# A graph attention layer and a gated graph recurrence on one core: adjacency loaded with a cast to float16 and turned by transposing transfers, nodes counted (k p)

## Chip, cores and metric

One core of a Trainium2 chip. The metric is device time in microseconds (us) of the whole kernel, the median of several executions. Lower is better. The engines are named as in the profile: PE (TensorE, with PEld for its weight loads), DVE (VectorE), ACT (ScalarE), POOL (GpSimd) and SP (SyncE, which only issues transfers here).

## The reference

There are 32 sequences (graphs) of 512 nodes with 128 features; all share one 512 x 512 adjacency matrix of zeros and ones.

```
# layer 0: graph attention
h = relu(layernorm(x))
hw = h @ W;  e_src = hw @ a_src;  e_dst = hw @ a_dst
logits = leaky_relu(e_src[i] + e_dst[j], 0.2), masked by A[i, j] > 0
x = x + leaky_relu(softmax_j(logits) @ hw + b, 0.3)
# layer 1: five steps of a gated recurrence
h = relu(layernorm(x))
repeat 5 times:
    m = A @ h                       # in_matrix and out_matrix are both A
    z = sigmoid([m, m] @ w3.T + w3_b + h @ u3.T + u3_b)
    r = sigmoid([m, m] @ w4.T + w4_b + h @ u3.T + u3_b)
    v = tanh([m, m] @ w5.T + w5_b + (r * h) @ u5.T + u5_b)
    h = (1 - z) * h + z * v
x = x + h
```

## The kernel before

**Layout.** P is 128 partitions, N 512 nodes, K = 4 blocks of 128 nodes, D 128 features. A sequence lies in the local memory either by nodes (partition = a node of a block, `[P, K, D]`) or turned (partition = a feature, `[P, N]`). Nodes are counted "(p k)": partition p holds nodes 4p to 4p+3, so one load of `x` reads 2 KB in one piece for each partition. The adjacency is loaded in float32 as `a_sb` (L415), and must then be turned: `prepare_adjacency` (L487) makes each of four blocks by four PE transposes (L494) into one bank of the accumulator memory, and copies them as float16 to `adjT` (L503, ACT for even, DVE for odd blocks).

**Layer 0** (`layer0`, L769) for each sequence: a norm (statistics L621, aggregate L629, `pow` on POOL L650, then for sequence 0 centring and scaling on DVE, L659 and L665, and for others a relu with scale on ACT, L687); a turn of the normed features; the product `hp` with W and the two attention vectors (L812); exponentials (L818) and scaled rows (L825); `es`, the row of exponentials spread over all partitions (L847); `pt`, the masked weights (L897, reads `es` and `adjT`); the averages `av` (L928); division, bias, leak and sum with x (L955 to L982), giving `x1`; and a second norm, whose result is `hN` and its two float16 halves `hi` (ACT, L1014) and `lo` (DVE, L1012). Turns and spreads are made by PE for the first DIRECT = 4 sequences, and for the others by a DVE block transpose and transfers through HBM from POOL's queue (`blockwise`, L723).

**The recurrence** (`recurrence`, L1018) for each step: `m` is made of four float16 matmuls with `hi` and four with `lo` against `adjT` (L1037), then copied to `mT` (ACT, L1048); `gate_r` is two float32 matmuls (L1056, L1057), `tanh` of it (ACT, L1062), `rh` (DVE, L1069), `gate_z` one matmul into the same bank (L1077), tanh (L1089), the candidate `v` two matmuls (L1100, L1101), tanh (L1107), and the update on DVE in three steps (L1114, L1120, L1123). The new state is split again and its halves are turned by transposing transfers from SP (`crossed`, L1231, L1245). The last sequences end with PE transposes; the last step of the last two sequences ("near") and of the last one (`ending`, L1256) have forms of their own. In `ending` the candidate is made in two halves of 256 columns in one bank, and the result is turned and summed by PE: four matmuls of the kept part against a scaled negative identity (`minus`, L1276) and four of the new part against a scaled identity (`plus`, L1306), accumulated in another bank.

**The order of work.** No order is written by hand. Each piece of work is a `Task` with an engine, an estimated duration, a key (its priority), the tasks that it needs and the buffers that it takes (L70). `plan` (L88) runs through all tasks with the costs of `COST` (L42) and puts each engine's tasks into one fixed order, which the kernel then issues. A transfer's `lands` is the estimate from its issue to its arrival. Where PE has nothing to do by this plan, filler matmuls on constants (`idle`, L443, 68 in all) are put in. Each engine works strictly in its order; an instruction that waits holds up all behind it on its engine, and a load that waits holds up SP's queue.

**The start.** SP's queue: x of sequence 0, `a_dst`, the adjacency, x of 1 and 2, the weights (`load_rest`, L410), five bias columns, x of 3 and so on. ACT's queue: `gw` (W) and `a_src`, both as columns.

**Sizes that matter:** ten sequences have slots for their state at a time; `d`, the buffer of the update on DVE, has 2 copies; the `pow` of both norms is on POOL, in its order with the transfers that POOL issues.

Of the kernel before, what the change touches and what calls it, by code (L numbers as in the profile page):

```python
# [28 lines left out]
DIRECT = 4  # L29
SHORT = 0  # L30
# [6 lines left out]
ADJ_LANDS = 5600  # L37
HALVED = 1
NEAR = 2
# [10 lines left out]
LANDING = 5000  # L50
CROSSING, CROSSED = 1250, 1400
# [7 lines left out]
    "hv": 2, "d": 2, "way": 4, "turn": 4, "line": 4, "hiT": 3, "loT": 3,  # L59
# [229 lines left out]
def gat_then_gated_gnn_kernel(  # L289
# [26 lines left out]
    x_r = x.rearrange("b (p k) d -> b p k d", k=K)  # L316
    out_r = out.rearrange("b (p k) d -> b p k d", k=K)
# [26 lines left out]

    ident = const.tile([P, P], F32, name="ident")
# [36 lines left out]
    prep = fast.enter_context(tc.tile_pool(name="prep", bufs=1))  # L382
    a_sb = prep.tile([P, K, N], F32, name="a_sb")
    gw = prep.tile([P, D], F32, name="gw")
    gwT = prep.tile([P, D], F32, name="gwT")
    acols = prep.tile([P, 2], F32, name="acols")
    cols = prep.tile([P, 5], F32, name="cols")
    sums2 = prep.tile([P, 2], F32, name="sums2")
    half = const.tile([P, 2], F32, name="half")
    nc.vector.memset(half, 0.5)  # L390
    wa = prep.tile([P, 2], F32, name="wa")
    wide = {name: prep.tile([P, 2 * D], F32, name=name) for name in ("w3", "w4", "w5")}
# [15 lines left out]
    nc.scalar.dma_start(out=acols[:, 0:1], in_=g_asrc.rearrange("(d o) -> d o", o=1))  # L408

    def load_rest(name):  # L410
        if name == "a_dst":
            pin(nc.sync.dma_start(out=acols[:, 1:2], in_=g_adst.rearrange("(d o) -> d o", o=1)))
            return
        if name == "a":
            pin(nc.sync.dma_start(out=a_sb, in_=adj.rearrange("(p k) m -> p k m", k=K)))  # L415
            return
# [8 lines left out]
        nc.sync.dma_start(out=bias0, in_=g_b.partition_broadcast(P))  # L425
# [3 lines left out]
    a_dst_loaded = add("SP", [1], -9.85e9, lambda: load_rest("a_dst"), lands=2900)  # L429
    a_loaded = add("SP", [1], -9.8e9, lambda: load_rest("a"), lands=ADJ_LANDS)  # L430
    xs[1] = load_x(1, -9.7e9, 5000)
    xs[2] = load_x(2, -9.6e9, 5100)
    rest_loaded = add("SP", [1] * 6, -9.5e9, lambda: load_rest("rest"), (xs[2][1],), lands=3000)
# [27 lines left out]

    def issue():
        pin(nc.tensor.matmul(new(f_wa, "wa_ps")[:, 0:2], lhsT=gwT, rhs=acols, start=True, stop=True))

    t = add("PE", [256], soon, issue, (a_dst_loaded, t), (f_wa,), at=5000)
# [17 lines left out]

    adjacency = []

    def prepare_adjacency(c):

        f = Buffer("g", "bank")
        key = (0.2 * c - 3.8) * STEP

        def turn():
            at_ps = new(f, f"at_ps{c}")
            for k in range(K):
                pin(nc.tensor.transpose(  # L494
                    at_ps[:, ts(k, P)],
                    a_sb[:, k, :].rearrange("p (q c) -> p c q", c=K)[:, c, :],
                    ident,
                ))

        t = add("PE", [256] * K, key, turn, (a_loaded,), (f,), at=9900 if c > 1 else 0)  # L500
        engine, copy = ("DVE", nc.vector.tensor_copy) if c % 2 else ("ACT", nc.scalar.copy)
        adjacency.append(
            add(engine, [512], key, lambda: pin(copy(adjT[:, c, :], f.tile)), (t,), (f,))  # L503
        )

    for c in range(K):
        prepare_adjacency(c)


# [45 lines left out]
    late = 5 * (B - 3) * STEP  # L555

    def count(k):
        f = Buffer("d")

        def issue():  # L560
            pin(nc.vector.scalar_tensor_tensor(
                new(f, f"odd_{k}"), a_sb[:, k, :], 0.0, a_sb[:, k, :], ALU.not_equal,
                ALU.not_equal, accum_out=counts[:, k : k + 1],
            ))

        return add("DVE", [512], late, issue, (adjacency[-1],), (f,), at=late)

    def degree(k):
# [5 lines left out]
        return add("DVE", [512], late, issue, (adjacency[-1],), at=late)  # L574
# [25 lines left out]


    def relu_layernorm(dst, src, which, keys, needs, buffers, first):
# [52 lines left out]
        if first:  # L655

            def centre():
# [14 lines left out]
            t1 = add("DVE", [512], keys(2), centre, (t1,), buffers)  # L672
            return [add("DVE", [256], keys(3), scale(i), (t, t1), buffers) for i in range(2)]

# [24 lines left out]
    def transposed(dst, src, which, keys, needs, buffers, by_halves):  # L699

        f = Buffer("o", "bank")

        def turn(half):
            def issue():
                t_ps = f.tile or new(f, f"t_{which}")
# [5 lines left out]
        def copy(of):  # L711
            return lambda: pin(nc.scalar.copy(dst()[:, of], f.tile[:, of]))

        t = [add("PE", [256] * 2, keys(0), turn(i), (needs[i],), (*buffers, f)) for i in range(2)]
        if not by_halves:
            t = add("ACT", [512], keys(1), copy(slice(0, N)), t, (*buffers, f))
            return [t, t]
        return [
            add("ACT", [256], keys(1), copy(ts(i, N // 2)), (t[i],), (*buffers, f))
# [3 lines left out]
    def blockwise(dst, src, which, keys, needs, buffers, by_halves):  # L723
# [23 lines left out]
        for g in range(G):  # L747
            stores.append(add("POOL", [1], keys(1), store(g), (t,), (f, way),
                              lands=LANDING))
# [7 lines left out]
        return add("POOL", [1], keys(2), load, stores, (*buffers, way), lands=LANDING + 1500)  # L757
# [11 lines left out]
    def layer0(b):  # L769
# [7 lines left out]
        def keys(i):  # L777
            return begin + length * (base[0] + i) / parts
# [12 lines left out]
        turn = transposed if direct else blockwise  # L791
# [11 lines left out]
        def product(half):  # L803
# [12 lines left out]

            def exponentials():
                pin(nc.scalar.activation(  # L818
                    hw()[:, 2 * half : 2 * half + 2, D:], hp2()[:, :, D:], AF.Exp
                ))  # L820
# [576 lines left out]
```

## Time and profile before

| what | value |
|---|---|
| median of 3 executions | 1137.68 us (1136.31 to 1139.9) |
| the profiled execution's own time | 1136.34 us |
| its span in the trace | 1134.6 us |
| DVE, ACT, POOL busy | 77%, 58%, 31% of the span |
| f32 gate and candidate matmuls (five lines, L1056 to L1101) | 814.4 us of summed durations |
| f16 matmuls with `hi` and `lo` (L1037) | 322.6 us of summed durations |
| transfers, mean | 92 GB/s, 104.52 MB |
| load of x, 256 KB, issue to landing | 2.9 us |
| transposing transfer from SP, issue to landing | 2.6 us |
| load of the adjacency, 1024 KB | 5.5 us |

Durations of matmuls in the trace overlap, since they are pipelined, so their sum is larger than the span; distances between starts are what they cost. "Idle before" beside a group is the time its engine waited ahead of it, and the releaser is what ended the wait. Times in the timeline count from the span's start.

### The profile page before, as it was taken

The numbers are of one execution on the slowest core, as the hardware profiler recorded it, in microseconds if no ns is written. First come the engines' busy times: TensorE is split into PE (matmuls) and PEld (weight loads), VectorE is DVE, ScalarE is ACT, GpSimd is POOL, SyncE is SP. The second block draws the span as 40 slices with busy tenths as digits, with TensorE's granted clock in tenths as the row PEclk, the third lists the DMA queues.
The fourth block names the chain that finished last, engine by engine and source line by source line (L and its number), as shares of the span: only waits on it lengthen the run. The fifth ranks groups of instructions, "written<-read, shape, count | busy, mean of one in ns | idle before, by whom it ended". The sixth has DMA issues, their size and how long they took to land.

```text
span 1134.6 us, 14335 instructions
## 1 busy us (share of the span) xinstructions
PE 1127.7 (99%) x4334; PEld 592.6 (52%) x4334; DVE 875.4 (77%) x2002; ACT 661.5 (58%) x1299; POOL 351.5 (31%) x504
## 2 busy tenths in 40 slices
PE   9999999999999999999999999999999999999998
PEld 8655555455455545555544555555555554444444
DVE  7888968887687788879777777889888976745655
ACT  6756656645655565656566556665656564555553
POOL 4255432511431344244134214453544230100000
PEclk9999999999999999999999999999999999999999
DMA  3245453643444554355345345454655343331321
GB/s 108 57 88 112 84 108 84 126 88 84 105 81 102 85 121 93 86 120 106 89 102 107 73 100 103 111 101 114 117 116 103 75 76 84 47 74 29 84 74 67
DMA packets 188498, 104.52 MB, mean 92 GB/s; under 512 B 152192, under 2 KB 167680, under 8 KB 188288
## 3 DMA queue, kind: packets, MB, share of 16 engines
q1 hardware_dynamic: 170512, 66.57, 25.4%
q0 software_dynamic: 17472, 36.79, 17.6%
q8 instruction: 36, 0.59, 0.2%
q14 instruction: 46, 0.38, 0.1%
q10 hardware_dynamic: 432, 0.20, 0.1%
HBM read 39.46 MB, written 30.47 MB: 62 GB/s over the span
## 4 chain that ended last, share of the span: by engine, by line
PE 99%; DMA 0%; DVE 0%; SPq 0%; issue 0%; DVEq 0%
PE m L1037 24%; PE g L1077 12%; PE g L1057 12%; PE g L1056 12%; PE v L1101 12%; PE v L1100 12%; PE av L928 10%; PE hp L812 3%; DMA a_sb<-in_adj_dram 0%; PE idle L443 0%; PE at_ps L494 0%; PE t_b L707 0%; PE t_a L707 0%; PE es L847 0%; PE v_end L1288 0%; PE end L1306 0%
## 5 line engine op out<-in xcount | busy, mean ns | idle before, releaser
L1062 ACT ACTIVATE rs<-g,zrb 128x512 f32<-128x512 f32 x160 | 109.6, 685 | 122.7 <-PE g L1057 121.9
L1114 DVE SCALAR_TENSOR_TENSOR d<-hv,hT 128x512 f32<-128x512 f32 x158 | 108.2, 685 | 92.9 <-ACT hv L1107 91.9
L1107 ACT ACTIVATE hv<-v,vb 128x512 f32<-128x512 f32 x159 | 108.8, 684 | 106.6 <-PE v L1101 106.3
L1069 DVE SCALAR_TENSOR_TENSOR rh<-rs,hT 128x512 f32<-128x512 f32 x160 | 109.5, 685 | 71.2 <-ACT rs L1062 70.5
L1056 PE MATMUL g<-hT,u3T 128*128 128x512 f32 x320 | 163.4, 592 | 0.0
L1057 PE MATMUL g<-mT,w4sT 128*128 128x512 f32 x320 | 163.4, 592 | 0.0
L1077 PE MATMUL g<-mT,w3dT 128*128 128x512 f32 x320 | 162.8, 593 | 0.0
L1101 PE MATMUL v<-rh,u5hT 128*128 128x512 f32 x318 | 162.4, 592 | 0.0
L1100 PE MATMUL v<-mT,w5sT 128*128 128x512 f32 x318 | 162.4, 592 | 0.0
L1037 PE MATMUL m<-adjT,hi 128*128 128x512 f16 x640 | 161.9, 379 | 0.0
L1037 PE MATMUL m<-adjT,lo 128*128 128x512 f16 x640 | 160.7, 379 | 0.0
L650 POOL TENSOR_TENSOR rs_b<-ve_b,mhalf 128x4 f32<-128x4 f32 x32 | 36.9, 1154 | 384.2 <-DVE ve_b L630 161.4
L1089 ACT ACTIVATE zs<-g,zrb 128x512 f32<-128x512 f32 x160 | 109.4, 685 | 68.0 <-PE g L1077 66.7
L1048 ACT COPY mT<-m 128x512 f32<-128x512 f32 x160 | 92.9, 583 | 81.7 <-PE m L1037 79.1
L928 PEld LDWEIGHTS av<-hw,pt 128*128 128x128 f32 x1024 | 123.5, 191 | 21.1 <-issue 17.5
L928 PE MATMUL av<-hw,pt 128*128 128x129 f32 x1024 | 125.0, 275 | 0.1
L1123 DVE SCALAR_TENSOR_TENSOR hT<-d,hT 128x512 f32<-128x512 f32 x158 | 109.3, 692 | 11.9
L1237 ACT CAST hiT<-hT 128x512 f16<-128x512 f32 x128 | 78.9, 616 | 66.2 <-DVE hT L1123 64.2
L1037 PEld LDWEIGHTS <-hi 128*128 128x128 f16 x640 | 62.6, 98 | 98.6 <-issue 45.0
L1120 DVE SCALAR_TENSOR_TENSOR d<-zs,d 128x512 f32<-128x512 f32 x158 | 109.2, 691 | 5.2
L1037 PEld LDWEIGHTS <-lo 128*128 128x128 f16 x640 | 62.6, 98 | 90.5 <-issue 25.3
L1240 DVE TENSOR_TENSOR loT<-hT,hiT 128x512 f16<-128x512 f32 x128 | 87.6, 687 | 17.7 <-ACT hiT L1237 16.3
(141 smaller groups left out, 1351.7 us busy)
## 6 DMA issues: line engine op xcount, KB each, us to landing
x<-in_x_dram SPq DMA_DIRECT2D x32, 256.0 KB, 2.9
out_dram<-res SPq DMA_DIRECT2D x31, 256.0 KB, 2.3
turn_a<-blocks_a POOLq DMA_DIRECT2D x112, 64.0 KB, 2.7
h0T<-turn_a POOLq DMA_DIRECT2D x28, 256.0 KB, 4.0
es<-line POOLq DMA_DIRECT2D x28, 256.0 KB, 4.3
turn_b<-blocks_b POOLq DMA_DIRECT2D x112, 64.0 KB, 2.6
hT<-turn_b POOLq DMA_DIRECT2D x28, 256.0 KB, 3.9
way<-blocks SPq DMA_DIRECT2D x28, 256.0 KB, 2.3
```

The costliest lines, as they stand in the source:

```text
L928: pin(nc.tensor.matmul(avs()[:, i, :], lhsT=f_pts[c].tile[:, ts(2 * part + i, P)], rhs=hw()[:, c, : D + 1], start=start, stop=(c == K - 1) ...
L1037: pin(nc.tensor.matmul(f_m.tile, lhsT=part[:, k, :], rhs=adjT[:, k, :], start=(first and k == 0), stop=(not first and k == K - 1),))
L1056: pin(nc.tensor.matmul(g, lhsT=u3T, rhs=hT, start=True, stop=False))
L1057: pin(nc.tensor.matmul(g, lhsT=w4sT, rhs=f_mT.tile, start=False, stop=True))
L1062: pin(nc.scalar.activation(new(f_r, f"rs_{b}_{step}"), f_g.tile, AF.Tanh, bias=rb, scale=0.5))
L1069: pin(nc.vector.scalar_tensor_tensor(new(f_rh, f"rh_{b}_{step}"), f_r.tile, 1.0, hT, ALU.add, ALU.mult))
L1077: pin(nc.tensor.matmul(f_g.tile, lhsT=w3dT, rhs=f_mT.tile, start=False, stop=True, skip_group_check=True))
L1089: pin(nc.scalar.activation(new(f_z, f"zs_{b}_{step}"), f_g.tile, AF.Tanh, bias=zb, scale=0.5))
L1100: pin(nc.tensor.matmul(v, lhsT=w5sT, rhs=f_mT.tile, start=True, stop=False))
L1101: pin(nc.tensor.matmul(v, lhsT=u5hT, rhs=f_rh.tile, start=False, stop=True))
L1120: pin(nc.vector.scalar_tensor_tensor(d, f_z.tile, 1.0, d, ALU.add, ALU.mult))
L1123: pin(nc.vector.scalar_tensor_tensor(hT, f_d.tile, 0.5, hT, ALU.mult, ALU.add))
```

## The change

Parts that concern the start:

- Nodes are counted "(k p)": partition p of block k holds node 128k + p, for `x`, `out` and the adjacency. A load of x then reads four pieces of 512 B for each partition instead of one of 2 KB.
- POOL issues, ahead of everything else it does, two loads of the adjacency with a cast to float16 (`a16`). SP then turns each block by a transposing transfer straight into `adjT`. The 16 PE transposes and the four copies go. The float32 adjacency `a_sb` is loaded late, since only the check of its values uses it.
- `pt` of a half waits for its two blocks only.
- The weights and bias loads stand behind the four transposing transfers in SP's order; bias0 moves to ACT's queue. The two attention vectors come as rows (`avecs`), and PE makes columns of them (`ac_ps`).
- For sequence 0 (`UNSCALED`) the norm's factor is left out of the features, and put into the exponentials' scale and into the row weights; the two halves of the turn and of `es` take a bank each.

Parts that concern the rest:

- `DIRECT` is split: 4 sequences for the first turn (`DIRECT_A`), 3 for `es` and for the second turn. Sequence 3 takes the transfers for these two.
- `SHIFT` adds offsets to the keys of some groups of layer 0 and of some steps, so the order moves; expected landings of POOL's transfers are shorter (`STORE_LANDS`, `SPREAD_LANDS`); `d` has 3 copies.
- `x1` of sequence 3 is summed on POOL (`JOIN_POOL`). For the "near" sequence `keep` takes a step on ACT, and `twice` is on POOL.
- `ending` has two pieces with a bank each, and the result is turned by four PE transposes; the scaling is in the last DVE step. The wait of the last but one candidate on the last gate_z goes (`Z_AHEAD`).

```diff
+    prep = fast.enter_context(tc.tile_pool(name="prep", bufs=1))
+    a16 = prep.tile([P, K, N], F16, name="a16")
+    rows = adj.rearrange("(k p) m -> p k m", k=K)
+    for i in range(2):
+        pin(nc.gpsimd.dma_start(out=a16[:, ts(i, K // 2), :], in_=rows[:, ts(i, K // 2), :]))
...
-    x_r = x.rearrange("b (p k) d -> b p k d", k=K)
+    x_r = x.rearrange("b (k p) d -> b p k d", k=K)
...
     xs = {0: load_x(0, -9.9e9, 3200)}
-    a_dst_loaded = add("SP", [1], -9.85e9, lambda: load_rest("a_dst"), lands=2900)
-    a_loaded = add("SP", [1], -9.8e9, lambda: load_rest("a"), lands=ADJ_LANDS)
-    xs[1] = load_x(1, -9.7e9, 5000)
-    xs[2] = load_x(2, -9.6e9, 5100)
-    rest_loaded = add("SP", [1] * 6, -9.5e9, lambda: load_rest("rest"), (xs[2][1],), lands=3000)
+    xs[1] = load_x(1, -9.8e9, 3500)
+    def turn_adjacency(k):
+        return lambda: pin(nc.sync.dma_start_transpose(
+            out=adjT[:, :, ts(k, P)], in_=a16[:, k, :]
+        ))
+    adjacency = [
+        add("SP", [1], -9.7e9 + k, turn_adjacency(k), at=TURN_AT[k], ns=CROSSING, lands=CROSSED)
+        for k in range(K)
+    ]
+    xs[2] = load_x(2, -9.7e9 + 1.5, 2500)
+    xs[2][1].at = TURN_AT[1] + 100
+    rest_loaded = add("SP", [1] * 5, -9.5e9, lambda: load_rest("rest"), lands=2500, at=TURN_AT[3] + 100)
...
+    u = add("PE", [256] * 2, soon, issue, (), (f_ac,), at=4100)
+    u = add("ACT", [1], soon, lambda: pin(nc.scalar.copy(acols, f_ac.tile[:, 0:2])), (u,), (f_ac,))
...
+    a_loaded = add("SP", [1], late - 60 * STEP, lambda: load_rest("a"), at=late - 60 * STEP, lands=9000)
...
-            return add("DVE", [of.stop - of.start], key, issue, (t, adjacency[c]),
+            return add("DVE", [of.stop - of.start], key, issue,
+                       (es_made[half], made[c // 2], *adjacency[of.start // P : of.stop // P]),
                        (f_es, f_hw, f_pts[c]))
...
-            return begin + length * (base[0] + i) / parts
+            return begin + length * (base[0] + i) / parts + SHIFT.get((b, base[0]), 0) * STEP
...
+        key += SHIFT.get((b, step, "step"), 0) * STEP
...
         def twice():
-            pin(nc.vector.scalar_tensor_tensor(
-                f_d.tile, f_hv.tile, LIFT, f_d.tile, ALU.mult, ALU.subtract
-            ))
+            pin(nc.gpsimd.tensor_tensor(f_d.tile, f_hv.tile, f_d.tile, ALU.subtract))
...
             def turn():
-                for k in range(two * i, two * i + two):
-                    pin(nc.tensor.matmul(
-                        f.tile[:, ts(k, P)], lhsT=f_p.tile[:, ts(k, P)], rhs=plus, start=False,
-                        stop=True, skip_group_check=True,
-                    ))
+                for k in range(ks.start, ks.stop):
+                    pin(nc.tensor.transpose(
+                        f.tile[:, ts(k - ks.start, P)], f_d.tile[:, ts(k, P)], ident
+                    ))
```

The first two transposing transfers read the first casting load, the other two the second: `TURN_AT = (4800, 6000, 7200, 8400)` are the times (ns) that the plan gives them, not waits.

## The prediction

> **What bounds the kernel now.** I read the busy table, the 40 slices and the chain of waits first, then the waits of TensorE (PE), then the timeline of both ends.
>
> ```profile
> PE 1127.7 (99%) x4334; PEld 592.6 (52%) x4334; DVE 875.4 (77%) x2002; ACT 661.5 (58%) x1299; POOL 351.5 (31%) x504
> PEclk9999999999999999999999999999999999999999
> PE 99%; DMA 0%; DVE 0%; SPq 0%; issue 0%; DVEq 0%
> ```
>
> PE carries 99% of the chain at full clock. The waits of PE over the whole span are short:
>
> ```profile
> PE at_ps L494 <- DMA a_sb<-in_adj_dram: 1.1, 1, 1.1
> PE idle L443 <- PEq L1384: 0.8, 1, 0.8
> PE end L1306 <- DVE gated L1299: 0.2, 1, 0.2
> ```
>
> So from 7.2 us on PE never stands still: the time is the sum of its matmuls, plus the start, plus what follows the last one. A busy PE isn't useful work, though: 68 filler matmuls (L443) are in it, 30 of them before 7.22 us. Both ends in the timeline:
>
> ```profile
> 1.66 0.42 SPq L415 DMA_DIRECT2D a_sb<-in_adj_dram  x1
> 7.22 0.75 PE L494 MATMUL at_ps<-ident,a_sb 128*128 128x128 f32 x4 [1.12 <-DMA a_sb<-in_adj_dram]
> 11.23 0.88 DVE L897 SCALAR_TENSOR_TENSOR pt<-es,hw,adjT 128x256 f32<-128x256 f32 x2
> 12.62 2.43 DVE L897 SCALAR_TENSOR_TENSOR pt<-es,hw,adjT 128x256 f32<-128x256 f32 x6
> 24.17 0.69 DVE L1012 TENSOR_TENSOR lo<-hN,hi 128x512 f16<-128x512 f32 x1
> 25.14 1.03 PE L1037 MATMUL m<-adjT,lo 128*128 128x512 f16 x4
> ...
> 1118.84 1.02 PE L1057 MATMUL g<-mT,w4sT 128*128 128x512 f32 x2
> 1128.65 1.16 PE L1306 MATMUL end<-plus,gated 128*128 128x128 f32 x8 [0.15 <-DVE gated L1299]
> 1130.63 0.81 SPq L1322 DMA_DIRECT2D out_dram<-res  x1
> ```
>
> The adjacency lands at 7.2 us, the first masked weights `pt` follow at 11.2 us, the first recurrence product of sequence 0 is whole only with its `lo` part at 25.14 us. The last store is issued at 1130.63 us, 4.0 us before the span's end.
>
> **What the Trainium skill says.** "DMA: Bandwidth & Descriptors", section SWDGE vs HWDGE vs iDMA: a cast needs GpSimd's software queue, a transpose SP's or ACT's hardware queue. Every transpose of this trace is on SP; no cast is in it. The same page, Anatomy of one DMA, prices a software DMA at 2.0 us plus bytes/436e3: 2.6 us for 256 KB, where the trace has 4.0 (h0T) and 4.3 (es), so I take it as a lower bound. "TensorE: Matmul & The Clock Gate", Part 1: after an idle window of about 3.4 us PE drops to half clock; here 1.1 us of idleness near 7 us left the clock at 1.00. "GPSIMD Engine Reference", section 3.1: 2.6 cycles an element in a two-input operation, an estimate of 1.1 us for 512; the trace has only 0.45 us for 128 columns.
>
> **The change part by part.** One pass of a small f32 matmul costs PE 0.11 us, an av matmul (two passes) 0.223, a 512-column f32 one 0.86, four f16 ones 0.86 (all from start-to-start distances in the timeline).
>
> *Work taken from PE.* 16 transposes of the adjacency (1.76 us, but they lay between 7 and 11.6 us, when PE waited for others and took fillers), 4 `es` and 4 `t_b` transposes of sequence 3 (0.88 us), and in the ending 8 two-pass products for 4 one-pass transposes (16-4 passes, 1.32 us).
>
> *The start, where the adjacency sets the pace.* (a) POOL issues two casting loads of 512 KB first of all; its 256 KB rows take 0.6 to 0.8 us each, so `ident` comes near 4 us, when `gw` lands (3.98 before): nothing lost. (b) Landing of the first half: no row shows a cast, so bounds. Early: an issue of 0.8 us after 0.74 and 2.9 us as for x, 4.4 us. Late: a cast at half rate or a slow first software DMA, 9 us. Taken: between 2 and 8 us the DMA engines are full at 380 to 390 GB/s; x0, x1, gw, bias0 and this half are 1.18 MB, 3.1 us from about 2.2 us on, so 5.3 us; the second half 1.4 us later, 6.7. (c) SP's queue then waits in order: transpose 0 at 5.3, transpose 1 at 6.5 (1.2 us each by the rows of L1245), landing 2.6 us after issue, 9.1; x2 at 7.7; transposes 2 and 3 at 8.1 and 9.3, landing at 11.9. Behind them stand the 5 weight and 5 bias loads, from 10.5 to 14.9 us instead of 3.1 to 10.4; they land by about 18. POOL's weight sums and `vb` stand ahead of the pow of norm b0, which comes at 18.8: just covered; with a later adjacency both move together. (d) The other inputs of `pt` are early: x0 lands at 3.7, the statistics end at 5.1, the unscaled centring needs no pow, so `es` is there by 7.7; ac_ps and its copy put 0.6 us into the wrow chain (5.4 to 6.0), under that cover. (e) VectorE: `pt` of half 0 from 9.2 (four of 0.40) to 10.8, the statistics of x2 that stand in its order there, 1.4 us, to 12.2, half 1 to 13.8. Before, the last ended at 15.05: 1.25 us gained. (f) Then VectorE works without a pause: norm b0, 4.85 us (4.45 before, where the two halves interleave, plus four exposed latencies of 0.1), to 18.7; `pt` of sequence 1, 2.7; two of sequence 2, 1.4; twice rsum and o, 1.5; one more pt, 0.7; leak, 0.7; then `lo` of sequence 0, from 25.7 to 26.4. Before it was ready at 24.9: its place behind others gives the gain back, and PE starts m's lo part at 26.4, 1.3 us later.
>
> *But more of the rest is done by then.* In the order of the changed program the part behind that point has 10 av matmuls fewer (2.23), 6 `es` (0.66) and 4 `t_b` transposes (0.44), the ending's 1.32, and 12 fillers fewer that cost time (1.28): 5.9 us. Before, 1104.7 us lie between 25.14 and the last matmul's end, so the last would end at 26.4+1098.8=1125.2 without gaps.
>
> *Gaps in the middle.* The order of many steps is moved (`SHIFT`), and slack changes. The tightest place I find: gate_z of sequence 5, step 0, waits for rs, which stands on ACT behind hN of sequence 6. From rsum of sequence 6 to that rs the rows give 8.8 us (o and leak 1.5, x1 with two others between 1.9, statistics 1.4, pow 1.1, nb 0.2, four relus 1.6, tanh 0.8, hand-overs 0.3), with 11.2 us of matmuls for cover; VectorE, 8 to 9 tenths busy there, comes to it 2 to 3 us late, so about 1 us is lost. Bounds for all such places 0 and 4 us; I take 1.6.
>
> *The ending.* From the end of gate_r of sequence 30 (1119.70 before): h_29, gate_r 31, gate_z 30, v_30, gate_z 31 take 5.6 us, the two pieces of v_31 with a filler 1.83, tanh 0.64, two 256-column VectorE steps 0.9, transposes 0.4, then res_30 stands ahead on VectorE until 9.65, two results 0.8: the store goes out at +10.5, before at +10.93. POOL's `twice` (1.1 to 1.4 us against 0.69) is done 0.5 us before PE wants it. That gate_r ends 8.2 us of matmuls before the last, at 1125.2-8.2+1.6=1118.6, so the last store is at 1129.1 against 1130.63: 1.5 us less.
>
> *At nothing:* x and out in pieces of 512 B, SP's issue having slack (rows of way, 512 B pieces, land in 2.0 us); the late load of a_sb (counts only at 886 us); JOIN_POOL once, POOL being busy 31%; the crossing of sequence 3 by POOL's DMA, two more chains of about 11 us with sequence 3 due later. If a cover fails, 0.3 to 1 us each.
>
> Sum: span 1133.1 against 1134.6, execution 1134.8 against its own 1136.34; that one is 1.3 us under the median of 1137.68, so the median becomes 1136.2.
>
> **The rivals.** *Early adjacency (faster by over 0.3%).* Landing at 4.4 us brings 0.9 us, no gaps 1.6, together 1133.7. For it: the queue is empty at 0.74 us. Against: DMA is full from 2 to 8 us.
> *Slow cast (slower).* One mechanism: the first transposing load waits on SP for the casting DMA, and `pt`, norm b0 and `lo` follow one to one, since VectorE has no pause behind them. It costs 1 us for each us after 5.3; past 6.8 us the change loses, past about 10 us by over 0.3%. At 9.5 us: 1140.4. For it: software DMAs of 256 KB, a quarter of the adjacency, already take 4.0 and 4.3 us here. Against: nothing in the trace shows a cast to be slow.
> *Gaps in the middle (slower).* ACT and VectorE wait in order behind relus and pow; 7 us of gaps instead of 1.6 give 1141.6. For it: the shifts are many and PE has almost no slack to lose unnoticed. Against: VectorE and ACT are 77% and 58% busy.
> *Cold clock.* PE idles near 8.5 to 9.7 and 12 us; if it throttles, work to about 16 us runs at half speed, some 3 us: 1139.
>
> **How the numbers follow.** A measurement of this kernel tells 0.3% (3.4 us) from no change. The forecast as worked, within 3.4 us of 1137.68: 0.54. Early adjacency: 0.14. Slow cast 0.14, gaps 0.12, cold clock 0.06; the slower ones count as slower, since a small one of each is in the forecast. So faster 0.14, same 0.54, slower 0.32. The range takes in a landing from 4.4 to 9.5 us and gaps from 0 to 5 us: 1133.2 to 1141.8.
>
> **What would show it.** Right: the first transposing load at 5 to 6 us, `pt` from about 9.2, m's lo part near 26.4, PE waits of 1 to 2 us in the middle with rs as their cause, the last store 0.4 us earlier after gate_r. Wrong: a16 after 7 us, PE clock under 1 in the first slices, or waits of over 4 us on rs, rh or hi.

## The result and the profile after

The changed kernel takes 1140.48 us (median of 13 executions, 1138.87 to 1144.09) against 1137.11 us for the kernel before on the same chip (13 executions). The ratio is 1.0029, with a 95% interval of 1.0017 to 1.0040: about 3 us slower, where 1136.2 had been forecast. Executions of either kernel come in two kinds, with the granted clock of TensorE at 0.999 or more or at 0.995 to 0.998, the second some 3 us longer (before: 1136.4 and 1140.1 us, medians over one chip's executions), so medians of two chips can't be set side by side, and the ratios, each against the kernel before on the same chip, stand in their place. A ratio is taken over the executions of both kernels; it is not the quotient of the two medians.

The profiled execution of the changed kernel is its slowest of 13: 1144.09 us, span 1142.3, 3.6 us above the median; that of the kernel before, 1136.34, lies 0.8 us under its median. So these profiles show where time is lost, and more of it than the median loses. First the changed kernel's page: busy time of each engine, granted clock in 40 slices, shares of the chain that ended last.

```profile
PE 1129.0 (99%) x4302; PEld 591.8 (52%) x4302; DVE 875.9 (77%) x2006; ACT 665.6 (58%) x1300; POOL 360.1 (32%) x518
...
PEclk8999999999999999999999999999999999999999
...
PE 91%; DMA 4%; DVE 2%; POOL 1%; issue 1%; ACT 0%; SPq 0%; DVEq 0%; POOLq 0%
```

PE still reads 99% busy, but the chain no longer runs through it alone: transfers carry 4%, where they carried 0%. And the first slice of the clock is an 8. PE's waits over the span (what was waited for, us in total, times, longest):

```profile
PE av L1000 <- DVE pt L967: 5.6, 3, 3.3
PE g L1134 <- DMA hT<-turn_b: 1.0, 1, 1.0
PE idle L475 <- PEq L1455: 0.8, 1, 0.8
PE v_end L1379 <- DVE kept L1373: 0.6, 1, 0.6
PE m L1115 <- DMA lo<-loT: 0.6, 1, 0.6
PE m L1115 <- DMA hi<-hiT: 0.5, 2, 0.3
```

Of this, 3.3 us are at the start, beside the first 0.8 us, which the kernel before has too. Another 4.4 us stand between 35 us and the ending, where the list of the kernel before has no wait: 2.3 us for `pt` (it waits in turn for `es` and `h0T`, which come through HBM), 1.0 for `hT`, 1.1 for `hi` and `lo`. The start and the last stores in the timeline (start, duration, engine, line, operation; in brackets the idle time before it and what ended it):

```profile
1.26 1.59 POOL L366 DMA_DIRECT2D a<-in_adj_dram  x2 [0.82 <-POOLq L1455]
...
8.40 2.60 SPq L455 DMA_TRANSPOSE adjT<-a  x2
...
12.34 1.66 DVE L967 SCALAR_TENSOR_TENSOR pt<-es,hw,adjT 128x256 f32<-128x256 f32 x4 [3.09 <-DMA adjT<-a]
...
12.97 2.92 PE L1000 MATMUL av<-hw,pt 128*128 128x129 f32 x12 [3.27 <-DVE pt L967]
...
30.57 0.69 DVE L1086 TENSOR_TENSOR lo<-hN,hi 128x512 f16<-128x512 f32 x1
...
31.51 1.03 PE L1115 MATMUL m<-adjT,lo 128*128 128x512 f16 x4
...
1137.51 0.42 ACTq L1392 DMA_DIRECT2D out_dram<-res  x1
1137.84 0.37 SPq L1392 DMA_DIRECT2D out_dram<-res  x1
```

The first transposing transfer leaves at 8.40 us, because the cast half lands 7.1 us after its issue. `pt` follows at 12.34, after VectorE waited 3.09 us for it; PE stood still for 3.27 us; and `lo` of sequence 0 is used at 31.51 us instead of 25.14. In the windows of 2 us from 12 us on, the granted clock reads 0.58, 0.50, 0.50 and 0.71. The Trainium skill's page "TensorE: Matmul & The Clock Gate", Part 1, has an idle window of about 3.4 us after which PE drops to half clock; the 3.3 us here agree. Over all runs the length of one idle stretch doesn't decide it: 3.4 us in e8 left the clock at 1.00, while 0.50 followed on 2.3 us in e2 and on 1.1 us in e13.

The difference of the two profiled executions, 1142.3 - 1134.6 = 7.7 us, can be laid out by place:

| stretch | before | after | difference |
|---|---|---|---|
| span's start to m's `lo` part of sequence 0 | 25.14 | 31.51 | +6.4 |
| from there to the end of gate_r of sequence 30 (1119.70; 1126.72) | 1094.56 | 1095.21 | +0.65: waits +4.4, work -3.75 |
| from there to the last store's issue (1130.63; 1137.84) | 10.93 | 11.12 | +0.2 |
| from there to the span's end | 3.97 | 4.46 | +0.5 |

So work did go, and two groups of waits more than took its place. The medians differ by 3.4 us, less than half of this. The experiments ask what makes each group.

### The profile page after: what moved, and what is told of

It is laid out like the page before. It is cut to its first block, busy times and chain, and to the rows that moved or that the text cites. A ratio compares the mean times of both kernels' runs of the same rounds, so it can differ in the third digit from the quotient of the medians.

```text
span 1142.3 us, 14307 instructions
## 1 busy us (share of the span) xinstructions
PE 1129.0 (99%) x4302; PEld 591.8 (52%) x4302; DVE 875.9 (77%) x2006; ACT 665.6 (58%) x1300; POOL 360.1 (32%) x518
## 4 chain that ended last, share of the span: by engine, by line
PE 91%; DMA 4%; DVE 2%; POOL 1%; issue 1%; ACT 0%; SPq 0%; DVEq 0%; POOLq 0%
PE m L1115 22%; PE g L1155 11%; PE g L1134 11%; PE g L1135 11%; PE v L1179 11%; PE v L1178 11%; PE av L1000 10%; PE hp L852 2%; DMA es<-line 1%; DMA a<-in_adj_dram 1%; DMA turn_a<-blocks_a 1%; DMA lo<-loT 1%; POOL turn_b L779 0%; POOL line L938 0%; DMA x<-in_x_dram 0%
## 5 line engine op out<-in xcount | busy, mean ns | idle before, releaser
L1000 PEld LDWEIGHTS av<-hw,pt 128*128 128x128 f32 x1024 | 125.9, 194 | 28.0 <-issue 21.9
L1000 PE MATMUL av<-hw,pt 128*128 128x129 f32 x1024 | 127.6, 278 | 5.6 <-DVE pt L967 5.6
L967 DVE SCALAR_TENSOR_TENSOR pt<-es,hw,adjT 128x512 f32<-128x512 f32 (+1 forms) x132 | 90.8, 729 | 14.9 <-DMA es<-line 11.6
```

Source lines behind the costliest of these rows:

```text
L1000: pin(nc.tensor.matmul(avs()[:, i, :], lhsT=f_pts[c].tile[:, ts(2 * part + i, P)], rhs=hw()[:, c, : D + 1], start=start, stop=(c == K - 1) ...
```

## The experiments

All times are medians of 6 to 22 executions; the ratio is to the kernel before on the same chip, with its 95% interval. "Middle" means PE's waits between 35 us and the ending (0 for the kernel before, 4.4 for the changed one), "`lo` used" the start of m's `lo` part of sequence 0; both are read from one profiled execution of each run. The fences of code show only the lines that carry an edit; "..." marks what is left out.

| run | median us | ratio | `lo` used | middle |
|---|---|---|---|---|
| changed kernel | 1140.48 | 1.0029 [1.0017, 1.0040] | 31.51 | 4.4 |
| e1 turned by PE, (k p) | 1146.33 | 1.0065 [1.0047, 1.0084] | 28.4 | 7.0 |
| e2 fillers ahead of av | 1143.33 | 1.0046 [1.0028, 1.0064] | 32.4 | 2.4 |
| e3 cast on engines | 1143.72 | 1.0049 [1.0034, 1.0065] | 27.8 | 5.0 |
| e4 POOL loads float32 | 1140.69 | 1.0023 [1.0008, 1.0039] | 30.4 | 1.6 |
| e5 a16 ready | 1139.99 | 1.0018 [1.0004, 1.0031] | 27.9 | 3.0 |
| e6 x, out in 2 KB | 1141.72 | 1.0015 [1.0003, 1.0027] | 30.7 | 3.4 |
| e8 both | 1140.57 | 1.0020 [1.0009, 1.0030] | 28.8 | 4.5 |
| e9 no late load | 1140.87 | 1.0026 [1.0012, 1.0040] | 30.7 | 4.4 |
| e10 old landing times | 1142.64 | 1.0046 [1.0033, 1.0059] | 31.2 | 5.2 |
| e11 no SHIFT | 1144.27 | 1.0061 [1.0044, 1.0078] | 26.0 | 2.6 |
| e12 sequence 3 on PE | 1139.83 | 1.0017 [1.0008, 1.0026] | 27.9 | 1.0 |
| e13 old start | 1143.66 | 1.0053 [1.0041, 1.0065] | 27.8 | 4.0 |
| e14 old start, by rows | 1145.22 | 1.0064 [1.0045, 1.0083] | 28.4 | 5.8 |
| e15 old start, no SHIFT | 1141.40 | 1.0032 [1.0021, 1.0043] | 26.7 | 0.5 |
| e7 before, (k p) | 1139.84 | 1.0007 [0.9996, 1.0019] | 27.03 | 0 |
| e16 before, cast; bias0 behind | 1140.11 | 1.0022 [1.0014, 1.0030] | 28.62 | 0 |
| e17 before, cast; bias0 on ACT | 1140.77 | 1.0031 [1.0021, 1.0041] | 29.61 | 0 |
| e18 before, cast; bias0 ahead | 1138.99 | 1.0014 [1.0003, 1.0024] | 27.59 | 0 |

### First call: is it the cast?

My theory was that the casting transfer is slow. Four edits of the changed kernel:

```diff
 # e1_pe_turn: float32 by SP in two halves, turned by PE
-pin(nc.gpsimd.dma_start(out=a16[:, ts(i, K // 2), :], in_=rows[:, ts(i, K // 2), :]))
+pin(nc.sync.dma_start(out=a_sb[:, ts(i, K // 2), :], in_=rows[:, ts(i, K // 2), :]))
...
+pin(nc.tensor.transpose(at_ps[:, ts(c, P)], a_sb[:, k, ts(c, P)], ident))
...
 # e2_warm: 22 fillers into the bank of av, ahead of its first product
+pin(nc.tensor.matmul(f.tile[:, : 2 * P], lhsT=unit[:, :P], rhs=unit, start=True, stop=True))
 # e3_engine_cast: float32 by SP, cast on ACT and DVE, then the same transposing transfers
+pin(copy(a16[:, k, :], a_sb[:, k, :]))
 # e4_pool_f32: the same casts, float32 by POOL's queue
+pin(nc.gpsimd.dma_start(out=a_sb[:, ts(i, K // 2), :], in_=rows[:, ts(i, K // 2), :]))
```

> The changed kernel with its adjacency loaded as float32 by SP's hardware queue, in two halves right behind x0, and turned by 16 TensorE transposes with four copies out of PSUM; the rest of the change is kept. Theory (the casting transfer lands too late, the rest of the change is a gain): the first half is in SBUF by about 5 us, pt of half 0 starts before 8.5 us instead of 12.3, m's lo part near 25 us instead of 31.5, no throttled clock: median 1135 to 1136.5. Rival (waits on DMA landings in the middle and a worse order of the steps took the gain): the start moves, but gaps of over 4 us stay behind 31 us and the median is 1138 or more.

> The changed kernel with 22 filler matmuls (about 0.11 us each) put into TensorE's queue just ahead of the first av product, so that it idles about 1 us there instead of 3.3. Theory (the idle stretch throttles the clock in some executions, and matmuls are the bound by then): clock 1.00 from 12 to 20 us in every execution, median 1139 to 1139.8, no run above 1141.5. Rival (VectorE sets the pace there, the half clock costs nothing): median 1140.5 and a spread up to 1143 as before.

> The changed kernel with the adjacency loaded as float32 by SP's hardware queue in two halves behind x0, cast to float16 by four copies of 512 columns on ScalarE and VectorE (about 0.6 us each), and turned by the same transposing transfers. Theory (the casting transfer is what is late): first transposing transfer issued at 5.8 to 6.8 us instead of 8.4, first av near 10.5 instead of 13, median 1137.5 to 1138.8. Rival (the transposing transfers and their place in SP's queue are the cost): no transposing transfer lands much before 10.9, median 1140 or more.

> As the kernel with casts on ScalarE and VectorE, but the two float32 halves come by GpSimd's software queue, without a cast in the transfer. If the cast in the transfer is slow: a half lands 4 to 5 us after its issue at 1.3 us, so by about 6 us, and the time is near that of the kernel with the hardware queue. If the software queue itself is slow beside the hardware queues that fill the DMA engines: it lands 7 us after its issue as the casting one does, and the time is 1140 or more.

e4 answers the question that I had put wrongly. Its timeline, at the cast on ACT that waits for the float32 half:

```profile
1.27 1.59 POOL L368 DMA_DIRECT2D a_sb<-in_adj_dram  x2 [0.83 <-POOLq L1462]
...
8.32 0.62 ACT L463 CAST a<-a_sb 128x512 f16<-128x512 f32 x1 [2.77 <-DMA a_sb<-in_adj_dram]
```

Without a cast in the transfer the half lands at 8.3 us too; with it, it landed between 8.1 and 9.0 us in the changed kernel, e2, e6, e9 and e10. So nothing shows the cast to be what is late. The DMA view of the changed kernel, from 4 to 6 us (packets, MB, share of 16 engines; q0 is POOL's software queue, q1 SP's, q10 ACT's), shows what the half meets:

```profile
DMA packets 452, 0.33 MB, mean 163 GB/s; under 512 B 27, under 2 KB 452, under 8 KB 452
...
q0 software_dynamic: 223, 0.22, 75.4%
...
q1 hardware_dynamic: 156, 0.07, 13.0%
...
q10 hardware_dynamic: 73, 0.03, 6.5%
```

The DMA engines are full, and POOL's two halves have 75% of them. The 163 GB/s count what is written: the view has 256 KB for a half that is 512 KB as read. Counted as read, the window moved some 270 GB/s (an estimate: 0.22 MB twice, and 0.10 MB of others, in 2 us), near e4's 288 in float32; the kernel before moved 393. In the 2 us before, POOL's queue placed 8 packets only, while the hardware queue of x0 and x1 had 75%. And the two halves were mixed: at 8.3 us, just before the first half was whole, 0.50 of the 0.52 MB of both had been placed.

Not every execution mixes them. e11 and e12 (below) issue the same first loads, within 0.02 us of the same times; there the first half landed at 6.26 and 6.31 us, with only 0.29 to 0.30 MB of both placed. In e12:

```profile
6.31 2.61 SPq L455 DMA_TRANSPOSE adjT<-a  x2
```

What decides between the two isn't known. But with the same loads, the first half lands anywhere from 6.3 to 9.0 us, and where two runs with one trace each differ by less than this, their edits need not be the cause.

The Trainium skill, "DMA: Bandwidth & Descriptors", section Anatomy of one DMA, gives 2.0 us plus bytes/436e3, an estimate of 3.2 us for one half; these traces have 5.0 to 7.7 us after the issue, beside other loads, and the measurement decides.

The other three were misses as to time. e3 had its first transposing transfer at 6.67 us (5.8 to 6.8 expected) and `lo` used at 27.8, but 5.0 us of waits in the middle, and took 1143.7. e1 had `lo` used at 28.4 and 7.0 us in the middle. In both, other times at the start let the planner make another order, so their middle can't be set beside the changed kernel's. In e2 the fillers covered the first idle stretch, but PE then idled 2.3 us for `pt` of half 1, and the clock fell to 0.50 at 18 to 20 us instead: fillers at one place don't settle what the clock costs.

### Second call: order kept

The edits of this call leave the order of each engine as it is. e5 and e8 leave the adjacency out of the result, and e6 and e8 number the nodes of x and out otherwise than those of the adjacency.

```diff
 # e5_ready: a16 filled with ones at the start, casting loads into a tile that nobody reads
+nc.vector.memset(a16, 1.0)
-pin(nc.gpsimd.dma_start(out=a16[:, ts(i, K // 2), :], in_=rows[:, ts(i, K // 2), :]))
+pin(nc.gpsimd.dma_start(out=b16[:, ts(i, K // 2), :], in_=rows[:, ts(i, K // 2), :]))
 # e6_whole_rows: (e8_ready_whole has both)
-x_r = x.rearrange("b (k p) d -> b p k d", k=K)
+x_r = x.rearrange("b (p k) d -> b p k d", k=K)     # out_r too
 # e7_before_kp: the kernel before with (k p) for x, out and adjacency
-    a_sb[:, k, :].rearrange("p (q c) -> p c q", c=K)[:, c, :],
+    a_sb[:, k, ts(c, P)],
```

> The changed kernel in its own order on every engine, but a16 is filled with ones by VectorE at the start and the two casting loads go into a tile that nobody reads: the adjacency is left out of the result, its transfers are kept. Theory (the late adjacency is the loss): transposing transfers from about 2 us, pt of half 0 near 8.5 us, bounded by hw and es, m's lo part at 26 to 28 us instead of 31.5, median 1135 to 1137. Rival (gaps behind the start took the gain, or the start is bounded by x1 and x2, which come in pieces of 512 B): median above 1139.

> The changed kernel in its own order, but x is read and out is written with nodes counted (p k), 2 KB in one piece for each partition as before the change; the adjacency stays as it is, so that the result belongs to a permuted graph. Theory (pieces of 512 B cost nothing, SP and the DMA engines have slack): median 1140 to 1141, as the changed kernel. Rival (the pieces slow x0, x1 and x2 at the start and every landing in the middle by their number of packets): 1137 to 1138.5.

> The kernel before, in its own order, with nodes counted (k p) throughout: x, out and the adjacency in pieces of 512 B and 2 KB, the TensorE transposes read contiguous columns; the result stays the same. Theory (the pieces cost nothing): 1136.5 to 1137.5, no change. Rival (they slow the DMA engines): the adjacency lands after 8 us instead of at 7.2, PE waits in the middle appear, 1138.5 to 1141.

> Both edits on the changed kernel: a16 ready at the start (the adjacency is left out of the result) and x and out in pieces of 2 KB. If late adjacency and pieces are two costs that add: 1132 to 1134.5. If the pieces cost nothing: the same as with a16 ready alone. If neither is the loss: above 1139.

e5 missed its 1135 to 1137 by 3 us. With `a16` full at about 2 us, the timeline shows why:

```profile
3.03 3.58 SPq L457 DMA_TRANSPOSE adjT<-a  x2
...
7.28 3.00 SPq L457 DMA_TRANSPOSE adjT<-a  x2
...
10.81 1.66 DVE L969 SCALAR_TENSOR_TENSOR pt<-es,hw,adjT 128x256 f32<-128x256 f32 x4 [1.93 <-DMA adjT<-a]
```

The first two transposing transfers leave at 3.03 us and `pt` still waits for them until 10.81: they take 6.3 us to land (the median; 2.5 in the changed kernel, where they run behind the loads). An `a16` that is there from the start thus brings 1.5 us at `pt`, not 4; in e12, where the casting load filled it by 6.31 us, the transfers landed in 2.6 us and `pt` came earlier still, at 10.27. In the time no gain clear of the noise is left: 1.0018 against 1.0029, with intervals that overlap.

e6 shows no gain clear of the noise either, and `a16` lands no earlier (first transposing transfer at 8.97 us); nor does e8, which has both edits (1.0020). In e7 the layout alone moves the landing of `a_sb` from 7.2 to 8.93 us and `lo` from 25.14 to 27.03 us, and its profiled span is 2.2 us longer, without a wait in the middle; this is one execution of each. Its ratio, 1.0007 [0.9996, 1.0019], doesn't tell it from no change. So the layout's cost is between nothing and 2 us.

### Third call: the middle

Each undoes one part of the change, or of its work, in the changed kernel; in e10, e11 and e12 the planner makes a new order from it.

```diff
 # e9_no_late_load
-pin(nc.sync.dma_start(out=a_sb, in_=rows))
+pin(nc.sync.dma_start(out=a_sb[:, 0, :P], in_=rows[:, 0, :P]))
 # e10_landings
-STORE_LANDS, SPREAD_LANDS = 3500, 5000
+STORE_LANDS, SPREAD_LANDS = 5000, 6500
 # e11_no_shift
-SHIFT = {
...
+SHIFT = {}
 # e12_turn3
-DIRECT_A, DIRECT_E, DIRECT_B = 4, 3, 3
+DIRECT_A, DIRECT_E, DIRECT_B = 4, 4, 4
-JOIN_POOL = (3,)
+JOIN_POOL = ()
```

> The changed kernel in its own order, with the late load of 1 MB of adjacency near 866 us cut to 64 KB; the test for entries other than 0 and 1 then reads ones set at the start, so that most of this test is left out. Theory (the late load costs nothing): the wait of PE for hi or lo near 880 us stays, 0.3 to 1.5 us. Rival (the late load fills the DMA engines just when hi and lo of a step cross): the wait near 880 us is gone, the other waits stay, 0.3 to 1 us faster.

> The changed kernel with the planner's landing times of the bounces through DRAM as before the change (5000 and 6500 ns instead of 3500 and 5000). Theory (the shorter figures put users too close behind landings, which take up to 7 us where several meet): the waits for hT, h0T, es behind 35 us fall from 2 to 3 us to under 1, PE's idle time between 35 and 1130 us under 2 instead of 3 to 4.5, 1 to 2 us faster. Rival (the figures don't matter, the order that SHIFT makes does): idle 3 us or more, and the time as the changed kernel or slower.

> The changed kernel with an empty SHIFT, so that no step is moved by hand. Theory (the shifts bring their steps into an order without waits on engines, and the waits that remain are DMA's): the waits on rs, rh, pt in the middle rise, 1 to 3 us slower than the changed kernel. Rival (the shifts make the waits, as my gaps step had it): PE's idle time between 35 and 1130 us under 2, 1 to 3 us faster.

> The changed kernel with sequence 3's es and its second turn on TensorE again (8 transposes of 0.11 us more) and its join on VectorE, instead of by bounces through DRAM. Theory (its bounces cost nothing): 0.9 us more work on PE, the waits near 107 and 353 us unchanged, 0.5 to 1 us slower. Rival (two more chains of bounces crowd the DMA engines near 60 to 110 us): the wait for lo near 107 us goes and so does the loss, same time or up to 1 us faster.

The late load shows no cost: in e9 a wait near 880 us is there without it (1.6 us for `hi`), and the ratio, 1.0026, is that of the changed kernel within the noise. The premise of its rival was wrong too: the load leaves at 528.47 us, not near 866. The shorter landing times aren't the cause either: with the old ones (e10) the waits near 353 us are gone, others of 3.6 us near 880 and 1.3 us after it have come, and the ratio is 1.0046. SHIFT helps: without it the ratio is 1.0061 [1.0044, 1.0078], clear of the changed kernel's.

e12 is the one whose profile has fewer waits. PE's waits over its span:

```profile
PE av L1000 <- DVE pt L967: 2.1, 3, 1.6
PE m L1115 <- DMA hi<-hiT: 1.0, 1, 1.0
PE idle L475 <- PEq L1455: 0.8, 1, 0.8
PE v_end L1379 <- DVE kept L1373: 0.6, 1, 0.6
```

All of `pt`'s 2.1 us are at the start; of the 4.4 us in the middle 1.0 are left, for 8 more transposes on PE. Five profiles with the changed kernel's own order (e2, e5, e6, e8, e9) have 2.4 to 4.5 us there, so 1.0 is low; but it is e12's fastest execution of 20, and e4, which keeps the bounces of sequence 3, has 1.6. The ratio falls from 1.0029 to 1.0017 with overlapping intervals, and the quotient of the medians stays at 1.003, so a gain in time isn't shown. Where the waits stand, transfers crowd: in the changed kernel from 340 to 362 us (DMA busy share in 40 slices, in tenths)

```profile
DMA  7639918959993959688987994200858800007400
...
turn_a<-blocks_a POOLq DMA_DIRECT2D x4, 64.0 KB, 6.7
...
es<-line POOLq DMA_DIRECT2D x1, 256.0 KB, 7.2
```

the stores of a turn take 6.7 us to land and the spread of `es` 7.2, against medians of 2.9 and 4.3 over the span. Bounces of two sequences and the halves of three steps meet there. In the kernel before, the same window moves 91 GB/s instead of 120, and its spread takes 4.3 us. That crowding makes the waits is read from these landings; no run takes it away alone. Of a `lo` issued at 106.7 us the chain of waits shows 6.2 us on the way.

### Fourth call: both undone

```diff
 # e13_before_start: (p k), one load of a_sb by SP, 16 PE transposes, sequence 3 on PE
+pin(nc.sync.dma_start(out=a_sb, in_=rows))
...
 # e14_start_by_k: two loads, turned row by row (at_ps of k), old landing times
+pin(nc.tensor.transpose(at_ps[:, ts(c, P)], a_sb[:, i, :].rearrange("p (q c) -> p c q", c=K)[:, c, :], ident))
 # e15_start_no_shift: as e13, old landing times, and
...
+SHIFT = {}
```

> The changed kernel with nodes counted (p k), the adjacency loaded by SP as float32 in one piece and turned by 16 TensorE transposes as before the change, and sequence 3 wholly on TensorE; its unscaled first norm, SHIFT and ending stay. Theory (late adjacency and crowded landings are the whole loss): at lands near 7.2 us, PE's idle time between 35 and 1130 us under 2, median 1134.5 to 1136.5, at or under the kernel before. Rival (the rest of the change, unscaled norm, SHIFT and ending, loses too): 1138 or more.

> As the kernel with the old start, but the adjacency comes in two halves of 512 KB and is turned row by row, so that pt of half 0 needs the first half alone, and the planner's landing times are the old ones. Theory: first half by 5.5 us, second at 7.2, pt of half 0 before 10 us, median 1134 to 1136. Rival (pt is bound by es and hw, or by the statistics of x1 that stand ahead on VectorE): no gain over the one piece, 1136 or more.

> As the kernel with the old start, without SHIFT and with the old landing times. If SHIFT fits only the start that it was made for: this one is as fast as the kernel with the old start or faster, 1134 to 1136.5. If SHIFT helps whatever the start: 1 to 3 us slower than the kernel with the old start.

This was to be the version that beats both, and my theory fell: 1143.7, 1145.2, 1141.4. In e13 the adjacency is there at 7.8 us, but PE waits 2.4 us for `hi` between 35 and 100 us, and the clock was 0.58 from 8 to 12 us. Without SHIFT (e15) the waits in the middle shrink to 0.5 us. With the changed start SHIFT brings the ratio from 1.0061 to 1.0029 (e11 against the changed kernel), with the old start it takes it from 1.0032 to 1.0053 (e15 against e13, which differ in the landing times also). e14, which has the old landing times and SHIFT, is slower than e15 as well (1.0064 against 1.0032, intervals apart), but it also turns the adjacency otherwise. So SHIFT seems to fit only the start that it was made for, and under it the cost of a part can't be read by undoing the part. What e15's profile has over that of the kernel before lies at the ends: PE stands still 2.0 us longer after 1130 us, 0.9 longer before 35, and has 1.0 us more of fillers.

### Last runs: the adjacency's new way in the kernel before

The kernel before has no waits in the middle, so its own order shows the start alone.

```diff
 # e16_before_cast: (k p); casting loads first on POOL; no PE transposes; bias0 where it was
+pin(nc.gpsimd.dma_start(out=a16[:, ts(i, K // 2), :], in_=rows[:, ts(i, K // 2), :]))
 # in load_rest, behind x of 0, 1 and 2, ahead of the weights:
+pin(nc.sync.dma_start_transpose(out=adjT[:, :, ts(k, P)], in_=a16[:, k, :]))
 # e17_bias_act, on ACT's queue behind a_src:
+nc.scalar.dma_start(out=bias0, in_=g_b.partition_broadcast(P))
 # e18_bias_sp, on SP just ahead of the transposing transfers:
+pin(nc.sync.dma_start(out=bias0, in_=g_b.partition_broadcast(P)))
```

> The kernel before, in its own order, with nodes counted (k p) and the adjacency as in the change: two casting loads on GpSimd's queue, four transposing transfers on SP behind x2, the float32 copy loaded late; the 16 TensorE transposes and their four copies are taken out. Nothing else of the change is in it. If the late adjacency costs by itself: first transposing transfer near 8.5 us, pt after 12 us instead of 11.2, m's lo part 3 to 5 us later than 25.1, no waits behind 35 us, and the time 1139.5 to 1142, 3 to 5 us over the kernel before. If the loss comes from the rest of the change: within 1 us of the kernel before in nodes counted (k p), so 1136.5 to 1139.

> The kernel before with the adjacency's new way alone (nodes counted (k p), casting loads, transposing transfers behind x2), and bias0 loaded early on ScalarE's queue as in the changed kernel. If the new way costs nothing once bias0 is out of SP's queue: no wait for bias0, m's lo part near 25.3 us, median 1136.5 to 1137.2. If the early broadcast competes with the casting loads on the DMA engines: first half in place at 8 to 8.5 us instead of 6.9, pt of half 0 after 12.5, m's lo part at 26.5 to 27.5, median 1137.5 to 1139.

> The same with bias0 on SP's queue, behind x2 and just ahead of the transposing transfers. If the place in SP's queue was the whole loss of the run with bias0 behind the transfers: m's lo part near 25.3 us, median 1136.5 to 1137.2, about 3 us under that run. If the layout of 512 B pieces costs by itself, as the run with the layout alone had m's lo part at 27.0 us: near 1138.5.

e16 has `lo` used 3.5 us later and a span 3.4 us longer (1138.0 against 1134.6), and most of it not for the adjacency's sake:

```profile
6.88 5.51 SPq L427 DMA_TRANSPOSE adjT<-a  x4
...
11.88 1.66 DVE L898 SCALAR_TENSOR_TENSOR pt<-es,hw,adjT 128x256 f32<-128x256 f32 x4
...
18.77 0.61 DVE L958 SCALAR_TENSOR_TENSOR o<-av,rsum,bias 128x128 f32<-128x128 f32 x2 [3.32 <-DMA bias<-in_L_gnn_b_dram]
```

Here the half is in place at 6.88 us, and `pt` starts 0.65 us later than before; what is late is bias0, which stands behind the transposing transfers. With bias0 early on ACT's queue, as the change has it (e17):

```profile
1.68 0.46 ACTq L415 DMA_DIRECT2D bias<-in_L_gnn_b_dram  x1
...
9.30 5.36 SPq L428 DMA_TRANSPOSE adjT<-a  x4
...
13.50 1.66 DVE L898 SCALAR_TENSOR_TENSOR pt<-es,hw,adjT 128x256 f32<-128x256 f32 x4
...
29.61 1.03 PE L1038 MATMUL m<-adjT,lo 128*128 128x512 f16 x4
```

the adjacency comes at 9.30 us, 2.4 us later, and nothing is won. With bias0 on SP ahead of the transfers (e18):

```profile
2.82 0.51 SPq L426 DMA_DIRECT2D bias<-in_L_gnn_b_dram  x1
...
7.15 5.38 SPq L428 DMA_TRANSPOSE adjT<-a  x4
...
11.96 1.66 DVE L898 SCALAR_TENSOR_TENSOR pt<-es,hw,adjT 128x256 f32<-128x256 f32 x4
...
27.59 1.03 PE L1038 MATMUL m<-adjT,lo 128*128 128x512 f16 x4
```

it comes at 7.15 us, and the same chip gives 1138.99 instead of 1140.77 us, ranges 1137.34 to 1140.26 and 1139.84 to 1142.78. So the place of bias0's broadcast is worth about 1.8 us. That it acts through the landing isn't shown: the 2.1 us between the two traces lie within the 2.7 us by which the changed kernel's landing differs between executions. The adjacency's new way, at its best here, is still 1.0014 [1.0003, 1.0024] of the kernel before: 1.6 us. The layout is in it, and alone (e7) it may cost as much, so how much of it is due to the loads and transposing transfers stays open. No ratio of any run is under 1; a version that beats the kernel before wasn't found. The changed kernel with bias0 moved to SP wasn't tried.

## Why the prediction was wrong

Its likeliest case was "no change", 1136.2 us; the outcome is 1.0029, 4.3 us over it in the median. That the median still lies inside the range is in part luck: the range has room for a landing at 9.5 us, but for another reason, and it leaves out that late landing and gaps come together, which by its own figures for 9.5 us and gaps of 5 us makes 1143.8. Against the profile taken, which is the slowest execution, its span of 1133.1 is 9.2 us short: 5.1 at the start, 3.0 between there and gate_r of sequence 30, 0.6 in the ending and 0.5 behind the last store.

*Work taken from PE*: holds roughly. Behind m's `lo` part 3.75 us of work went up to gate_r of sequence 30, where its figures make 5.9 - 1.3 = 4.6.

*The start, (b) the landing of the first half* is the step that failed. The prediction took 1.18 MB at 380 GB/s, in order of issue, and found 5.3 us; measured were 8.40 in the profile, and 6.3 to 9.0 over the executions that begin with the same loads. Two terms were wrong. The rate: the kernel before has 393 and 378 GB/s from 4 to 8 us, but 231 from 2 to 4. x0, x1, gw, bias0 and both halves, 1.70 MB, were there by about 8.4 us; from the prediction's 2.2 us on this is an estimate of 275 GB/s, and at this rate the first half alone, in turn, would land at 6.5 us, near the 6.3 of e11 and e12. The order: where the packets of the halves were mixed, as in the profile, the first half was whole only when nearly all of both was placed, 1.9 us later. The bound of 9 us and the rival of a slow cast (1140.4 for 9.5 us) had the right size, but the cast isn't shown to be the cause: e4 lands as late without one.

How much of the 3.4 us in the median this landing makes isn't shown. With `a16` there from the start (e5) the ratio is still 1.0018 [1.0004, 1.0031]; in the order of the kernel before, with nothing else of the change in it, the new way costs 1.0014 at its best (e18).

*(c) to (f)*: the transposing transfers landed 2.5 us after issue, as taken; `pt` followed at 12.34, 3.1 us late, as the landing; norm b0 didn't wait for POOL's weight sums. "One to one" held up to there. `lo` was 5.1 us late instead of 3.1. From `pt` to `lo` the prediction had 17.2 us; e5, e8, e9 and e12, whose clock stayed at 1.00, have 17.1 to 17.8, and the profile 19.2. So most of the other 2 us go with the halved clock of 12 to 20 us, which the prediction had as its rival of 0.06 and priced at 3 us. The idle stretch that it feared at 12 us came at 9.7 to 12.97.

*Gaps in the middle* failed by size and by cause: 1.6 us for rs behind hN on ACT, bounds 0 to 4. The trace has 4.4 us, none on rs; all are landings of `es`, `h0T`, `hT`, `hi` and `lo`. "The crossing of sequence 3", costed at nothing "with sequence 3 due later", may be a part of it: undone, it leaves 1.0 us in one profile (e12).

*The ending*: +11.1 us instead of +10.5, so no gain. PE waited 0.6 us for `kept`, because a VectorE step that takes 0.69 us in the kernel before took 1.73 (see below); the prediction priced `twice` on POOL without what it does to VectorE.

*At nothing*: the late load shows no cost (e9), nor do 512 B pieces in the changed kernel (e6); in the kernel before the layout may cost up to 2 us (e7).

## What to carry to other kernels

An early transfer is priced by what else is in the DMA engines then and by how queues mix, not by bytes over the best rate seen; where two loads are issued together and the first is needed first, reckon with the landing of both. Before a landing in one trace is taken for the effect of an edit, look how far it differs between executions that begin alike. Transfers that replace TensorE work move it into a shared resource: look where several of them land together (here 6.7 and 7.2 us against medians of 2.9 and 4.3). Where an order is fitted to one start by hand-set offsets, test a part in an order that has no waits of its own, with the order kept.

## What the runs showed of the hardware

A VectorE operation waited for one on GpSimd. In the changed ending, from the timeline:

```profile
1133.15 1.26 POOL L1218 TENSOR_TENSOR kept<-hv,kept 128x512 f32<-128x512 f32 x1 [133.53 <-DVE hv L1215]
...
1133.23 1.73 DVE L1345 SCALAR_TENSOR_TENSOR kept<-zs,hT 128x512 f32<-128x512 f32 x1 [0.17 <-ACT zs L1167]
```

The same step takes 0.69 us in the kernel before, where POOL is at rest; here it starts 0.08 us after POOL's and ends 0.55 us after POOL's end. All fifteen profiles with the changed ending have the same 1.73 us. The Trainium skill, "SBUF — State Buffer", section Who interferes with whom, says so: VectorE and GpSimd share a pair of ports, which is an exclusive lock, and a VectorE instruction with two inputs in SBUF contends with a GpSimd one that reads SBUF. Moving `twice` to POOL thus took 0.69 us off VectorE, and cost it 1.04 us at the step behind, which sets the end.

Two software loads of half the adjacency, issued together beside the same other loads, landed in two ways in different executions: the first at 6.3 us (e11, e12) with 0.29 to 0.30 MB of both placed, or at 8.1 to 9.0 us (the changed kernel, e2, e9, e10) with 0.50 MB or more.

Transposing transfers of 128 KB landed 2.5 us after issue beside little else, 2.6 us (median) in e12, where they left at 6.31 us with the second casting half still coming, and 6.3 us (median) in e5, where they left from 3.03 us on, ahead of the casting loads' landing.
